# A second level of seven-product multiplication for two of the seven products of the values, in a fused cross-attention, self-attention and expert block

## The chip, the cores and the metric

The kernel runs on one core of a Trainium2 chip, in one launch, with all data in float32. The metric is the device time of one execution in microseconds (us); the number to compare is the median of three runs. The engines are PE (TensorE, with its weight loads as PEld), DVE (VectorE), ACT (ScalarE), POOL (GpSimd) and the DMA queues that SP feeds.

## What is computed

The reference is a block of three layers on 128 latent tokens of width 512, with a context of 12544 tokens of width 512. Cut to what matters here:

```python
# layer 1: quantised self-attention of the latents and cross-attention over the context
kvx = einsum('bsi,oi->bso', cond, w_kv_x)        # cond: 12544 x 512, w_kv_x: 2048 x 512
kx, vx = split(kvx, 2, axis=-1)                  # 8 groups of 128 each
kx = layernorm(kx.reshape(b, sc, 8, 128))
xout = gqa(qx, kx, vx)                           # 16 heads of 128, softmax over 12544 tokens
x = x + proj(concat(core, xout))
# layer 2: causal self-attention of the latents, 16 heads of 32
x1n = ln(ln(x)); x = x + softmax(mask(q k^T)) v Wo
# layer 3: 32 experts, the best 8 of each token, weighted
y = x + moe(ln(x))
```

Nearly all the work is keys and values of the context (`kvx`) and the attention over them.

## The kernel before, in words

**Chunks.** The context is taken in 25 chunks (`chunks`, `NCH`): 24 of 512 tokens and one of 256, which is number 12. For each chunk the kernel makes keys `KT` (8 groups of 128 rows by 512 tokens) and values `V` (4 tiles of 128 tokens by 1024 columns), then scores, an online softmax and outputs. The loop at L856 runs over the chunks. In the scores stage it goes through the eight groups: `scores` (L698: four matmuls per group, 128 x 256 each, copied from PSUM by ACT with the keys' norm as a factor, then a maximum by DVE), and with each group one step of the values of the same chunk. In the keys stage (`keys`, L425) it goes through eight steps of the keys of the next chunk, and after each the outputs of one group (`outputs`, L800).

**Seven products.** Keys and values are made by a multiplication of 2 x 2 blocks in seven products in place of eight. Tokens of a chunk are halved in number and in width (b11, b12, b21, b22), the weights likewise. `mix_tokens` (L284) makes the sums and differences of token blocks on POOL, four operations of 128 x 512 a chunk, one chunk ahead; `mix_weights` makes those of the weights once. Products are numbered by their place in `mixed_w` and `mixed[c]`. `unit` (L319) makes a quarter of the rows: bank `a` takes product 0, then 5, then 6, then 3 on top of each other, `b` takes 1, `c` takes 4 and then 2. ACT copies the sums out of `a` between (`held`: p1, u2, u3), DVE adds. Its four steps are

```python
mm(a, 0, True); p1 = held("p1"); mm(b, 1, True)      # d11 = b + p1
mm(a, 5, False); u2 = held("u2"); mm(c, 4, True)
mm(a, 6, False); u3 = held("u3")                     # d22 = c + u3
mm(a, 3, False); mm(c, 2, False)                     # d21 = a, d12 = c + u2
```

A unit of the values (`v_unit`, L371, matmuls at L378) has two matmuls of 128 x 128 by 512 columns per product; a chunk has two such units, so eight steps, one with each group of scores. A unit of the keys (`k_unit`, L351, matmuls at L359) has four matmuls of 256 columns per product, and there are two a chunk. The banks a, b, c come from `ps_kv`, three PSUM banks in a ring; scores and outputs share three banks of another pool.

**The norm of the keys.** After each unit of keys `k_sums` (L386) squares the unit's rows on ACT, two groups of heads at a time (128 x 1024), into one buffer `sq`, and DVE reduces each half (L395). `k_rstd` then makes the factors for the score copies (a matmul L407, DVE L412, a power on POOL L414).

**The softmax.** `maxima` (L849) runs after each step: at steps 4 and 8 `max_rows` makes the running maxima for four groups on DVE, and at 5, 6, 9 and 10 `spread` (L771) takes two groups: DVE spreads shift and rescale over the rows (L766), subtracts (L783), ACT takes Exp in place (L787), and POOL multiplies the running output `ol` by the rescale (L789) and adds the weights up (L797).

**Order.** Instructions are written in the order of the loops; the framework's planner reorders them within each engine's queue by its own estimate of when they can start. `tc.issue_after(x)` holds an instruction behind another. Each queue runs in order, and each instruction waits there for what it needs. Pools of tiles set which buffers are reused, and so which waits arise.

**The tail.** After the last chunk the outputs are normalised and projected (`proj`), then the self-attention follows (from about L1010): norm (`norm_rows`, L200), four transposes into one PSUM bank (`transposed`, L248), projections for q, v and k in this order, score products L1065 onto a mask already in PSUM, then for four blocks a maximum and a subtraction on DVE, Exp on ACT, transposes, a copy and the value products. `spin` (L931) issues small matmuls of 240 columns whose results nobody reads; the tail has some of these between steps. The router and the experts come last.

Of the kernel before, what the change touches and what calls it, by code (L numbers as in the profile page):

```python
# [17 lines left out]
P = 128  # L18
H = 512
# [26 lines left out]
def block_kernel(  # L46
# [153 lines left out]
    def norm_rows(dst, src, twice=False):  # L200

        st = small.tile([P, 6], F32, tag="st1", name="st1")
        mv = small.tile([P, 2], F32, tag="mv1", name="mv1")
        nc.vector.bn_stats(st, src)
        nc.vector.bn_aggr(mv, st)


        v = small.tile([P, 1], F32, tag="ve1", name="ve1")
        if twice:
            nc.vector.tensor_scalar(v, mv[:, 1:2], 1.0 + EPS, EPS * EPS, ALU.mult, ALU.add)  # L210
        else:
            nc.gpsimd.tensor_scalar(v, mv[:, 1:2], EPS, None, ALU.add)
        rs = small.tile([P, 1], F32, tag="rs1", name="rs1")
        powered[0] = nc.gpsimd.tensor_tensor(rs, v, mhalf[:, :1], ALU.pow).ins
        end = nc.vector.tensor_scalar(dst, src, mv[:, 0:1], rs, ALU.subtract, ALU.mult)
        return end.ins
# [31 lines left out]
    def transposed(pool, src):  # L248

        ps = pool.tile([P, 4, S], F32, tag="ps", name="ps_t")  # L250
        for k in range(4):
            turned[0] = nc.tensor.transpose(ps[:, k, :], src[:, k * P : (k + 1) * P], ident).ins
        return ps

# [48 lines left out]
    mixed, last_mm, added = {}, [None], [None]  # L303
# [15 lines left out]
    def unit(mm, view, d11, d12, d21, d22):  # L319
# [7 lines left out]
        def held(name):  # L327
            t = tmpk.tile([P, CH], F32, tag="u", name=name, bufs=3)
            nc.scalar.copy(view(t), va)  # L329
            return view(t)  # L330
# [54 lines left out]

    def k_sums(c, u):  # L386

        n = chunks[c][1]
        r = tmpk.tile([P, 4, CH // 32], F32, tag="sqr", name="sqr")
        for j in range(2):  # L390
            g = 4 * u + 2 * j
            sq = tmpk.tile([P, 2, CH], F32, tag="sq", name="sq", bufs=1)
            nc.scalar.activation(sq[:, :, :n], KT[:, g : g + 2, :n], AF.Square)  # L393
            for i in range(2):
                nc.vector.tensor_reduce(  # L395
                    r[:, 2 * j + i, : n // 32], sq[:, i, :n].rearrange("p (b i) -> p b i", i=32),
                    AX.X, ALU.add, apply_transpose=True,
                )
        return r
# [284 lines left out]

    olp = late.enter_context(tc.tile_pool(name="olp", bufs=1, side="right", reuse_waits="tile"))
# [10 lines left out]
    prob, mxr, mrun, shifts, lsum, summed = {}, {}, {}, {}, {}, [None]  # L696

    def scores(c, g):  # L698
# [4 lines left out]
        for t0 in range(0, nt, 2):  # L703
            ps = ps_so.tile([P, 2, HS], F32, tag="s", name="s_ps")
            for t in range(t0, t0 + 2):
                end = nc.tensor.matmul(  # L706
                    ps[:, t - t0, :], lhsT=KT[:, g, t * P : (t + 1) * P],
                    rhs=qxT[:, 2 * g : 2 * g + 2, :], start=True, stop=True,
                )
            for t in range(t0, t0 + 2):  # L710
                nc.scalar.activation(  # L711
                    s[:, t, :], ps[:, t - t0, :], AF.Copy, scale=rs[:, t : t + 1]
                )
# [57 lines left out]
    def spread(c, j):  # L771
# [5 lines left out]
        if c:  # L777
            alb = tmp.tile([P, 2, HS], F32, tag="al", name="al", bufs=3)
            to_all(alb, al)
        for a in range(2):  # L780
            g = 2 * j + a
            s = prob[g]
# [4 lines left out]
            nc.scalar.activation(s[:, :nt, :], s[:, :nt, :], AF.Exp, scale=scale)  # L787
            if c:
                nc.gpsimd.tensor_tensor(  # L789
                    ol[g], ol[g], alb[:, a, None, :].to_broadcast([P, 2, HS]), ALU.mult  # L790
# [58 lines left out]
    def maxima(c, i):  # L849

        if i in (4, 8):
            max_rows(c, i // 2 - 2, 2)
        if i in (5, 6, 9, 10):
            spread(c, i // 4 * 2 - 2 + (i - 1) % 4)

    for c in range(NCH):  # L856
# [3 lines left out]
        todo = parts(v_unit(c, v) for v in range(0 if c else 1, chunks[c][1] // HS))  # L860
        for g in range(G):
# [10 lines left out]
            if g == 2 and c + 1 < NCH:  # L872
                with tc.issue_after(summed[0] if c else made):
                    for step in mix_tokens(c + 1):
                        step()

# [11 lines left out]
    with ExitStack() as rest:  # L888
# [7 lines left out]
        stream += [w.rearrange("(k p) o -> p k o", p=P) for w in (aWq, aWv, aWk, aWo)]  # L896
# [113 lines left out]
        with tc.tile_pool(name="po_s", bufs=1, space=PSUM, reuse_waits="tile") as pss:  # L1010
            sps = pss.tile([S, 4, 4, S], F32, name="sps")
            with tc.issue_after(end):
# [8 lines left out]
            pt = transposed(pps, xnn)  # L1021
            xT = post1.tile([P, NK, S], F32, name="xT1")
            for k in range(NK):
                end = nc.vector.tensor_scalar(
                    xT[:, k, :], pt[:, k, :], col("g", k), col("b", k), ALU.mult, ALU.add
# [5 lines left out]
            def project_T(nm, bias, by):  # L1031
                w = next_w()
                ps = pps.tile([P, NK, S], F32, tag="ps", name="ps_qk")
                for j in range(NK):
                    for k in range(NK):
                        nc.tensor.matmul(
                            ps[:, j, :], lhsT=w[:, k, j * P : (j + 1) * P], rhs=xT[:, k, :],
                            start=k == 0, stop=k == NK - 1,
                        )
# [3 lines left out]
                return t  # L1043

            qa = project_T("bq", lambda j: bqs[:, j : j + 1], 1.0 / math.sqrt(AD))
            w = next_w()
            ps = pps.tile([S, H], F32, tag="ps", name="ps_v")
            for k in range(NK):
                nc.tensor.matmul(ps, lhsT=xT[:, k, :], rhs=w[:, k, :], start=k == 0, stop=k == NK - 1)

            va = post1.tile([S, AH, AD + 1], F32, name="va")
            with tc.issue_after(summed[0]):
                nc.gpsimd.memset(va[:, :, AD:], 1.0)
            nc.vector.tensor_tensor(
                va[:, :, :AD], ps.rearrange("s (h d) -> s h d", d=AD),
                bvo[:, 0, :].rearrange("s (h d) -> s h d", d=AD), ALU.add,
            )
            ka = project_T("bk", lambda j: col("bk", j), 1.0)

            for j in range(4):
                for a in range(4):
                    r = slice(a * AD, (a + 1) * AD)
                    end = nc.tensor.matmul(  # L1065
                        sps[:, a, j, :], lhsT=qa[r, j, :], rhs=ka[r, j, :], start=False, stop=True,
                        skip_group_check=True,
                    ).ins
            n = AH // 2 * (AD + 1)
            rest_ps = pss.tile([S, H], F32, name="ps_av2")  # L1070
# [4 lines left out]
            unread = rest_ps[:, H - 240 :]  # L1075

            end = spin(unread, end, 4)
            for a in range(4):
# [3 lines left out]
                nc.vector.tensor_tensor(  # L1082
                    pe, sps[:, a], mx[:, :, None].to_broadcast([S, 4, S]), ALU.subtract
                )
                nc.scalar.activation(pe, pe, AF.Exp)
                with tc.issue_after(end):
                    pt = transposed(pps, pe.rearrange("p j t -> p (j t)"))
                if a in (0, 3):
                    end = spin(unread, turned[0], 1)
# [10 lines left out]
            for i in range(2):  # L1100
# [5 lines left out]
                )  # L1106
            with tc.issue_after(end):
                pt = transposed(pps, av.rearrange("s h d -> s (h d)"))
            end = spin(unread, turned[0], 1)
            avT = post1.tile([P, 4, S], F32, name="avT")  # L1110
            nc.scalar.copy(avT[:, 0:2, :], pt[:, 0:2, :])
            nc.vector.tensor_copy(avT[:, 2:4, :], pt[:, 2:4, :])
# [13 lines left out]
        with tc.tile_pool(name="mo_t", bufs=2, space=PSUM) as mps, tc.tile_pool(  # L1126
# [3 lines left out]
            norm_rows(xn, x2)  # L1130
            with tc.issue_after(end):
                pt = transposed(mps, xn)
            xT = post1.tile([P, NK, S], F32, name="xT2")
            nc.vector.tensor_copy(xT[:, 0:2, :], pt[:, 0:2, :])
            nc.scalar.copy(xT[:, 2:4, :], pt[:, 2:4, :])
# [118 lines left out]
```

## Time and profile before

| | |
|---|---|
| median of 3 runs | 2180.73 us (2180.57 to 2181.01) |
| the profiled execution | 2182.46 us, its span 2180.7 us |
| mean granted TensorE clock | 0.999 |
| one whole chunk, scores to scores (188.50 to 265.51) | 77.01 us |
| its scores stage (419.55 to 458.06, another chunk) | 38.51 us |
| last chunk's outputs begin | 1964.93 us |
| first matmul behind the last projection, tail | 2002.83 us |
| DMA, mean over the span | 44 GB/s |

A row of the page's groups reads: line, engine, operation, output<-inputs, shape, count, then busy time, the mean of one in ns, and the idle time of the engine ahead of it with the instruction that ended most of it. In a timeline the first number is the start and the second the length of a run of like instructions; one matmul of the code shows as two records. In a windows row the first pair is the stretch, then its length, busy time (and instructions) of PE, PEld, DVE, ACT and POOL, the granted TensorE clock, and DMA. A wait reads: who waited for whom, total us, times, longest.

### The profile page before, as it was taken

The page shows a single profiled execution, that of the slowest core. Times are in us where ns is not written, and L with a number is a line of the kernel's source. Part 1 is how long each engine was busy: PE and PEld are TensorE (multiplying, and loading weights), DVE is VectorE, ACT ScalarE, POOL GpSimd, SP SyncE. Part 2 cuts the span into 40 slices and gives each one's busy share as a digit, 9 for nine tenths or more (in the row PEclk, how much of TensorE's full clock was granted, in tenths as well). Part 3 has the DMA queues.
Part 4 walks back from the last instruction along what each step waited for, and adds up shares of the span by engine and source line. Part 5 has one row for each costly group of instructions (what it writes and reads, how often), then busy time and mean ns, then how long its engine had stood idle before and what let it go on. Part 6 is the DMA issues. An engine that isn't in the chain of part 4 may idle for free.

```text
span 2180.7 us, 23767 instructions
## 1 busy us (share of the span) xinstructions
PE 2155.4 (99%) x8671; PEld 1526.5 (70%) x8671; DVE 1307.5 (60%) x2336; ACT 896.3 (41%) x1687; POOL 1092.9 (50%) x1172
## 2 busy tenths in 40 slices
PE   8999999999999999999999999999999999999999
PEld 3667766776776677677776776777677677666554
DVE  8775575567457557646676567557556745757311
ACT  3444454344345434444444345444434434441211
POOL 5233664564476457447574475466456446633000
PEclk9999999999999999999999999999999999999999
DMA  9300000000000000000000000000000000008593
GB/s 319 111 20 1 20 20 1 20 20 20 1 20 20 0 20 20 10 1 20 20 20 17 3 20 20 1 20 20 1 20 20 20 1 20 1 1 276 189 283 116
DMA packets 71221, 95.48 MB, mean 44 GB/s; under 512 B 3136, under 2 KB 39488, under 8 KB 71104
## 3 DMA queue, kind: packets, MB, share of 16 engines
q1 hardware_dynamic: 70816, 93.92, 13.0%
q8 instruction: 68, 1.11, 0.2%
q14 instruction: 49, 0.40, 0.1%
q10 hardware_dynamic: 288, 0.04, 0.0%
HBM read 93.69 MB, written 0.26 MB: 43 GB/s over the span
## 4 chain that ended last, share of the span: by engine, by line
PE 93%; DVE 4%; ACT 1%; DMA 1%; issue 1%; POOL 0%; SPq 0%; POOLq 0%; ACTq 0%; DVEq 0%
PE a_ps L359 15%; PE a_ps L378 15%; PE o_ps L805 15%; PE s_ps L706 15%; PE c_ps L359 8%; PE c_ps L378 7%; PE gu_ps L1169 4%; PE b_ps L378 4%; PE b_ps L359 4%; PE moe_acc L1190 2%; PE ps_p L508 1%; DVE s L783 1%; DVE mxr L717 1%; PE ps_core L668 1%; PE ps_proj L915 1%; DVE m_new L744 1%
## 5 line engine op out<-in xcount | busy, mean ns | idle before, releaser
L797 POOL TENSOR_TENSOR ol<-ol,s 128x256 f32<-128x256 f32 x764 | 550.9, 729 | 58.0 <-ACT s L787 20.3
L711 ACT ACTIVATE s<-s_ps,krs 128x256 f32<-128x256 f32 x784 | 324.1, 471 | 181.4 <-PE s_ps L706 179.2
L414 POOL TENSOR_TENSOR krs<-kve,mhalf 128x16 f32<-128x16 f32 (+1 forms) x50 | 142.8, 2856 | 498.6 <-DVE kve L412 498.6
L789 POOL TENSOR_TENSOR ol<-ol,al 128x512 f32<-128x512 f32 x192 | 242.4, 1273 | 288.8 <-DVE al L766 288.8
L706 PE MATMUL s_ps<-qxT,KT 128*128 128x256 f32 x1568 | 373.1, 381 | 1.6 <-ACT s L711 1.6
L805 PE MATMUL o_ps<-s,V 128*128 128x256 f32 x1568 | 370.7, 379 | 0.0
L706 PEld LDWEIGHTS s_ps<-qxT,KT 128*128 128x128 f32 x1568 | 295.7, 190 | 103.8 <-issue 68.4
L717 DVE TRANSPOSE_TENSOR_REDUCE mxr<-s 128x32 f32<-128x1024 f32 (+1 forms) x200 | 242.4, 1212 | 187.8 <-ACT s L711 184.9
L805 PEld LDWEIGHTS o_ps<-s,V 128*128 128x128 f32 x1568 | 297.1, 190 | 40.8 <-issue 0.5
L787 ACT ACTIVATE s<-s 128x1024 f32<-128x1024 f32 (+1 forms) x200 | 208.1, 1041 | 156.0 <-DVE s L783 150.2
L783 DVE TENSOR_TENSOR s<-s,b_ps 128x1024 f32<-128x1024 f32 (+1 forms) x200 | 230.3, 1171 | 0.0
L329 ACT COPY u<-a_ps 128x512 f32<-128x512 f32 (+1 forms) x198 | 114.5, 578 | 248.8 <-PE a_ps L359 202.3
L378 PE MATMUL a_ps<-wkv,ctx 128*128 128x512 f32 x392 | 186.2, 597 | 1.7 <-DMA ctx<-in_ctxT 1.7
L359 PE MATMUL a_ps<-ctx,wkv 128*128 128x256 f32 (+1 forms) x800 | 185.7, 375 | 1.2 <-POOL ol L789 1.2
L810 DVE TENSOR_TENSOR ol<-ol,o_ps 128x256 f32<-128x256 f32 x192 | 79.7, 415 | 175.6 <-PE o_ps L805 173.5
L359 PEld LDWEIGHTS a_ps<-ctx,wkv 128*128 128x128 f32 x800 | 150.0, 190 | 30.9 <-issue 12.1
L395 DVE TRANSPOSE_TENSOR_REDUCE sqr<-sq 128x16 f32<-128x512 f32 (+1 forms) x200 | 128.0, 678 | 57.4 <-ACT sq L393 57.3
L393 ACT ACTIVATE sq<-KT 128x1024 f32<-128x1024 f32 (+1 forms) x100 | 104.0, 1040 | 134.4 <-DVE KT L348 91.2
L348 DVE TENSOR_TENSOR KT<-c_ps,u 128x512 f32<-128x512 f32 (+1 forms) x50 | 34.0, 681 | 140.0 <-PE c_ps L359 140.0
L378 PEld LDWEIGHTS a_ps<-wkv,ctx 128*128 128x128 f32 x392 | 74.9, 191 | 54.5 <-issue 47.2
L359 PE MATMUL a_ps<-mix,wkv 128*128 128x256 f32 (+1 forms) x400 | 97.4, 386 | 3.4 <-ACT u L329 3.4
L378 PE MATMUL a_ps<-wkv,mix 128*128 128x512 f32 x196 | 94.6, 605 | 0.0
(227 smaller groups left out, 2775.0 us busy)
## 6 DMA issues: line engine op xcount, KB each, us to landing
ctx<-in_ctxT SPq DMA_DIRECT2D x23, 1024.0 KB, 5.0
gu<-in_w SPq DMA_DIRECT2D x32, 384.0 KB, 4.8
gu<-in_v SPq DMA_DIRECT2D x32, 384.0 KB, 5.5
dn<-in_w SPq DMA_DIRECT2D x16, 768.0 KB, 5.5
w<-in_wprojT SPq DMA_DIRECT2D x8, 1024.0 KB, 5.7
w<-in_wqxT SPq DMA_DIRECT2D x4, 1024.0 KB, 11.2
w<-in_wqT SPq DMA_DIRECT2D x4, 1024.0 KB, 6.0
wkv<-in_wkvT SPq DMA_DIRECT2D x8, 256.0 KB, 8.2
```

The costliest lines, as they stand in the source:

```text
L359: nc.tensor.matmul(ps[:, j * h : (j + 1) * h], lhsT=w[:, k, (2 * u + j) * D : (2 * u + j + 1) * D], rhs=x[:, k, :], start=first and j == k ...
L378: last_mm[0] = nc.tensor.matmul(ps, lhsT=x[:, k, v * P : (v + 1) * P], rhs=w[:, k, H : 2 * H], start=first and k == 0, stop=k == 1, skip_g ...
L395: nc.vector.tensor_reduce(r[:, 2 * j + i, : n // 32], sq[:, i, :n].rearrange("p (b i) -> p b i", i=32), AX.X, ALU.add, apply_transpose=True,)
L414: nc.gpsimd.tensor_tensor(rs[:, :, :nt], ve[:, :, :nt], mhalf.rearrange("p (g t) -> p g t", g=4)[:, :, :nt], ALU.pow,)
L706: end = nc.tensor.matmul(ps[:, t - t0, :], lhsT=KT[:, g, t * P : (t + 1) * P], rhs=qxT[:, 2 * g : 2 * g + 2, :], start=True, stop=True,)
L711: nc.scalar.activation(s[:, t, :], ps[:, t - t0, :], AF.Copy, scale=rs[:, t : t + 1])
L717: nc.vector.tensor_reduce(mxr[g // 4][:, g % 4, :nt, :].rearrange("p t k -> p (t k)"), s[:, :nt, :].rearrange("p t (k i) -> p (t k) i", i=32),
L783: nc.vector.tensor_tensor(s[:, :nt, :], s[:, :nt, :], ps[:, a, None, :].to_broadcast([P, nt, HS]), ALU.subtract,)
L787: nc.scalar.activation(s[:, :nt, :], s[:, :nt, :], AF.Exp, scale=scale)
L789: nc.gpsimd.tensor_tensor(ol[g], ol[g], alb[:, a, None, :].to_broadcast([P, 2, HS]), ALU.mult)
L797: summed[0] = nc.gpsimd.tensor_tensor(ol[g][:, 1, :], first, s[:, t, :], ALU.add).ins
L805: end = nc.tensor.matmul(ps, lhsT=V[:, t, g * D : (g + 1) * D], rhs=s[:, t, :], start=t == 0, stop=t == nt - 1,)
```

## The change

For whole chunks other than the first (23 of the 25), the values are made by `v_chunk` in place of two `v_unit`s. Products 1 and 3 appear in one block of the result each. `v_chunk` makes both, for the chunk's two token tiles at once, by seven products of quarter blocks: per quarter product one matmul of 256 columns for product 1 and one for product 3, side by side in a bank. Their four steps run beside groups 0 to 3, and their results go to `V`. Then each of the two token tiles has the other five products in two steps beside groups 4 to 7, and DVE adds their sums to what stands in `V`. The quarter sums of the weights (`finer`, four POOL operations once) and of the tokens (`fx`, eight POOL operations on 128 x 128 a chunk, one buffer, issued in the code after group 4) are new.

To hold these tiles, `k_sums` squares one group of heads at a time (128 x 512) in a buffer of half the size, and the rescale tiles `al` have two buffers in place of three. `spread` is cut in two: the Exp, the rescale and the sums are now in `weigh`, which in chunks 0, 11 and 12 is held behind the last ACT copy at some places, or put off by one step.

In the tail the order of the projections is q, k, then two of v's four matmuls, the score products, and the other two of v; the bias add of v moves behind the first subtraction; three groups of transposes go to two banks in place of one (`transposed_halves`); six of the spins are dropped; and one step of `norm_rows` moves from POOL to DVE.

```diff
-            nc.gpsimd.tensor_scalar(v, mv[:, 1:2], EPS, None, ALU.add)
+            nc.vector.tensor_scalar(v, mv[:, 1:2], EPS, None, ALU.add)
...
+    def transposed_halves(tiles, src):
+
+        for i, ps in enumerate(tiles):
+            for k in range(2):
+                j = 2 * i + k
+                turned[0] = nc.tensor.transpose(
+                    ps[:, k, :], src[:, j * P : (j + 1) * P], ident
+                ).ins
+        return tiles
...
+    def mix_finer_tokens(c, eng):
+        t = finp.tile([P, 2, 4, P], F32, tag="fx", name=f"finer_{c}")
+        finer_x[c] = []
+        for i, x in enumerate((mixed[c][1], mixed[c][3])):
...
+            eng.tensor_tensor(t1, b12, b11, ALU.subtract)
+            eng.tensor_tensor(t2, b22, t1, ALU.subtract)
+            eng.tensor_tensor(t3, b22, b12, ALU.subtract)
+            eng.tensor_tensor(t4, b21, t2, ALU.subtract)
...
+    def v_chunk(c):
...
+        def fine(ps, n, first):
+            for i in range(2):
+                nc.tensor.matmul(
+                    ps[:, i * H // 2 : (i + 1) * H // 2], lhsT=xs[i][n], rhs=f[n][:, i, :],
+                    start=first and i == 0, stop=True, skip_group_check=True,
+                )
...
+        a, b = bank("fa_ps"), bank("fb_ps")
+        fine(a, 0, True)
+        p1 = held(a, "p1")
+        fine(b, 1, True)
+        nc.vector.tensor_tensor(to(0, 0), both(b), both(p1), ALU.add)
+        yield
+        fine(a, 5, False)
+        u2 = held(a, "u2")
+        d = bank("fc_ps")
+        fine(d, 4, True)
+        yield
+        fine(a, 6, False)
+        u3 = held(a, "u3")
+        nc.vector.tensor_tensor(to(1, 1), both(d), both(u3), ALU.add)
+        yield
+        fine(a, 3, False)
+        nc.scalar.copy(to(1, 0), both(a))
+        fine(d, 2, False)
+        nc.vector.tensor_tensor(to(0, 1), both(d), both(u2), ALU.add)
+        yield
+        for v in range(2):
...
+            t1, t2 = V[:, v, :], V[:, 2 + v, :]
+            a, d = bank("a_ps"), bank("c_ps")
+            mm(a, 0, True)
+            nc.vector.tensor_tensor(t1[:, :H], a, t1[:, :H], ALU.add)
+            mm(d, 4, True)
+            nc.scalar.copy(t2[:, H:], d)
+            yield
+            mm(a, 5, False)
+            u2 = held(a, "u2")
+            mm(d, 2, False)
+            nc.vector.tensor_tensor(t2[:, :H], d, u2, ALU.add)
+            mm(a, 6, False)
+            nc.vector.tensor_tensor(t2[:, H:], a, t2[:, H:], ALU.add)
+            added[0] = nc.vector.tensor_tensor(t1[:, H:], a, t1[:, H:], ALU.add).ins
+            yield
...
-        for j in range(2):
-            g = 4 * u + 2 * j
-            sq = tmpk.tile([P, 2, CH], F32, tag="sq", name="sq", bufs=1)
-            nc.scalar.activation(sq[:, :, :n], KT[:, g : g + 2, :n], AF.Square)
-            for i in range(2):
...
+        for j in range(4):
+            sq = tmpk.tile([P, CH], F32, tag="sq", name="sq", bufs=1)
+            nc.scalar.activation(sq[:, :n], KT[:, 4 * u + j, :n], AF.Square)
+            nc.vector.tensor_reduce(
...
-            alb = tmp.tile([P, 2, HS], F32, tag="al", name="al", bufs=3)
-            to_all(alb, al)
+            rescale[j] = tmp.tile([P, 2, HS], F32, tag="al", name="al")
+            to_all(rescale[j], al)
...
+    def weigh(c, j, after=None):
...
+            with tc.issue_after(after) if after else nullcontext():
+                nc.scalar.activation(s[:, :nt, :], s[:, :nt, :], AF.Exp, scale=scale)
...
+            last = copied[0]
+            if c == 0 and i == 6:
+                weigh(c, 0, last)
+            if c == NCH // 2 and i == 10:
+                weigh(c, 2, last)
+            spread(c, j)
+            if (c, j) in ((0, 0), (NCH // 2, 2)):
+                return
+            weigh(c, j, last if (c, j) in ((0, 3), (NCH // 2 - 1, 2)) else None)
...
+        if whole(c):
+            todo = v_chunk(c)
+        else:
+            todo = parts(v_unit(c, v) for v in range(0 if c else 1, chunks[c][1] // HS))
...
+                    if c == 0:
+                        mix_finer_weights(nc.gpsimd)
+            if g == 4 and c + 1 < NCH and whole(c + 1):
+                mix_finer_tokens(c + 1, nc.gpsimd)
...
-        stream += [w.rearrange("(k p) o -> p k o", p=P) for w in (aWq, aWv, aWk, aWo)]
+        stream += [w.rearrange("(k p) o -> p k o", p=P) for w in (aWq, aWk, aWv, aWo)]
...
+            with tc.issue_after(end):
+                end = v_part(range(2))
+            with tc.issue_after(end):
+                for j in range(4):
+                    for a in range(4):
...
+            with tc.issue_after(end):
+                end = v_part(range(2, NK))
...
-            end = spin(unread, end, 4)
...
+                if a == 0:
+                    with tc.issue_after(sub.ins):
+                        nc.vector.tensor_tensor(
+                            va[:, :, :AD], ps_v.rearrange("s (h d) -> s h d", d=AD),
+                            bvo[:, 0, :].rearrange("s (h d) -> s h d", d=AD), ALU.add,
+                        )
...
-                if a in (0, 3):
-                    end = spin(unread, turned[0], 1)
+                end = spin(unread, turned[0], 1) if a == 0 else turned[0]
...
-            end = spin(unread, turned[0], 1)
```

## The prediction

> **What bounds the kernel now.** I read the page first (busy shares, chain), then the timeline of PE over one whole chunk, then PE's waits, then ACT, DVE and POOL in the same chunk by timeline, groups and windows, and last the tail.
>
> ```profile
> PE 2155.4 (99%) x8671; PEld 1526.5 (70%) x8671; DVE 1307.5 (60%) x2336; ACT 896.3 (41%) x1687; POOL 1092.9 (50%) x1172
> PE 93%; DVE 4%; ACT 1%; DMA 1%; issue 1%; POOL 0%; SPq 0%; POOLq 0%; ACTq 0%; DVEq 0%
> ```
> TensorE is busy for all but 25 us, and 93% of the chain that ends last is PE. Ends of matmuls are modelled, so I take rates from starts:
>
> ```profile
> 419.55 1.89 PE L706 MATMUL s_ps<-qxT,KT 128*128 128x256 f32 x8
> 421.27 1.88 PE L378 MATMUL a_ps<-wkv,ctx 128*128 128x512 f32 x4
> 422.99 1.88 PE L378 MATMUL b_ps<-wkv,ctx 128*128 128x512 f32 x4
> 424.71 1.89 PE L706 MATMUL s_ps<-qxT,KT 128*128 128x256 f32 x8
> ```
> One matmul of the code is two records here. Start to start, four records of 512 columns take 1.72 us and eight of 256 take 1.72 us: 0.43 and 0.215 us a record. Half the columns cost half the time. The groups follow without a gap: PE is the bound, and in a normal chunk (419.55 to 496.57, 77.0 us) nothing else holds it. Only a few waits exist, none in a normal chunk:
>
> ```profile
> PE a_ps L359 <- ACT u L329: 3.4, 2, 2.3
> ...
> PE s_ps L706 <- ACT s L711: 1.6, 2, 1.3
> PE a_ps L359 <- POOL ol L789: 1.2, 1, 1.2
> ```
> By the timeline they lie in chunk 0 (1.26 and 1.13), in the turn from chunk 11 to 12 (1.22) and in chunk 12 (0.38 and 2.25), 6.2 us in all. The one put down to POOL has ACT's copy of u at its end (1005.14 to 1005.49, the product starts at 1005.64), behind an Exp.
>
> **The products.** A whole chunk's values are 2 units of 7 products of 2 matmuls of 512 columns. Products 1 and 3 go: 2 units x 2 products x 2 matmuls = 8 of 512 columns, 16 records x 0.43 = 6.88 us. The seven products of quarters are 7 x 2 matmuls of 256 columns: 28 records x 0.215 = 6.02 us. Saved 0.86, or 0.84 with the 1.715 a product that 445.75 to 449.18 gives for two; 23 chunks are whole and not the first: 19.3 us off the bound. That the small form runs at this rate is the row of the scores: same 128 rows, 256 columns, a new stationary tile for every matmul.
>
> **What feeds and empties them.** PE's two halves of the scores stage change length. Now:
>
> ```profile
> core 0: us, PE busy (x) PEld busy (x) DVE busy (x) ACT busy (x) POOL busy (x), PEclk, DMA share, GB/s
> 419.55:438.86 19.31, 19.31 (x70) 11.47 (x68) 10.33 (x15) 10.20 (x22) 2.90 (x1) 1.00 0.00 0
> 438.86:458.06 19.20, 19.19 (x62) 11.32 (x61) 16.87 (x28) 12.30 (x25) 12.98 (x16) 1.00 0.00 1
> ```
> After: heads 0 to 3 have 4 scores x 1.72 + 6.0 + 0.3 = 13.2 us, heads 4 to 7 have 4 x 1.72 + 10 products x 1.72 = 24.1 us. ACT's copies stay eight a chunk. DVE's adds go from six to eleven:
>
> ```profile
> L343 DVE TENSOR_TENSOR V<-c_ps,u 128x512 f32<-128x512 f32 x49 | 33.0, 673 | 5.8 <-ACT u L329 5.8
> L393 ACT ACTIVATE sq<-KT 128x512 f32<-128x512 f32 x4 | 2.5, 631 | 2.8 <-DVE sqr L395 1.8 <-DVE KT L348 1.0
> L797 POOL TENSOR_TENSOR ol<-ol,s 128x256 f32<-128x256 f32 x764 | 550.9, 729 | 58.0 <-ACT s L787 20.3
> ```
> 5 x 0.68 = 3.4 us of DVE, all in the second half: 16.9 + 3.4 = 20.3 of 24.1 us (84%, now 88%); the first half keeps 10.3 in 13.2 (78%). ACT has about 10.6 of 13.2 in the first half (80%, now 53%). Nobody exceeds PE, so the adds are counted at nothing; the cover is PE's longer second half, and without it they would cost up to 3.4 us a chunk. The tight places, one by one: product 5 waits for the add out of its bank, but product 4 and the next scores (3.44 us) lie between, against 0.68 plus one or two DVE operations of 1.2. Product 6 waits for the copy of u2 with only product 2 (1.72) between, against 0.15 + 0.58, or 1.79 with an Exp (1.06) ahead: 0.1 late at worst. The bank of the first unit's product 6 is next needed by product 4 of the second, 3.44 us on, against two adds of 0.68 and a subtraction of 1.19.
>
> The squares are the most exposed. Now:
>
> ```profile
> 399.36 1.06 ACT L393 ACTIVATE sq<-KT 128x1024 f32<-128x1024 f32 x1 [1.87 <-DVE KT L348]
> 402.16 1.06 ACT L393 ACTIVATE sq<-KT 128x1024 f32<-128x1024 f32 x1 [1.74 <-DVE sqr L395]
> 403.13 0.57 ACT L329 COPY p<-a_ps 128x512 f32<-128x512 f32 x1
> ```
> After, one buffer of half the size makes four squares and four reductions take turns: in chunk 12, where squares have 512 columns, square to reduction is 0.66 and reduction's end to the next square 0.10; with a reduction of 0.69 a turn is 1.45. Three turns and the last square (0.53) start p's copy at 399.36 + 4.88 = 404.24; it ends at 404.82. Product 5 that needs it starts at 405.34. Queued behind the squares on ACT are that copy and, at the chunk's turn, the scores' copies; PE waits for both. There the smaller products need p at about 424.7 against about 424.3. So 0 if the turns go as worked out, and up to 1.2 us a chunk if each waits for one more DVE operation. I take 0.13 us, near the computed slack: 3 us over 23 chunks. A gain is excluded here, since the chain only gets longer.
>
> POOL gets eight operations on 128x128 a chunk; none is in the trace; 729 ns for 256 columns and 1273 for 512 make about 0.46 (0.3 to 0.73), 3.7 us. They need the last small product of the chunk before (one buffer) and are read a chunk later. POOL now idles 10.2 us until 443.66, in front of the first rescale, so they cost nothing; in another place they would move the sums, which have 12.8 and 10.2 us of such idle time a chunk. The four weight sums (128x512, 5.1 us) come once, in a POOL gap of 45 us before 123. The Trainium skill speaks against this (SBUF — State Buffer, "SBUF: two separate sides"): a GpSimd operation and a VectorE operation with two SBUF inputs lock each other out for a whole instruction. The trace shows something like it: L749 on DVE took 0.19 us at 441.60 with POOL idle, and 0.70 at 461.07 beside POOL's sums; the three small ones behind it stayed at 0.19. By the rule four small DVE operations wait 0.46 each, 1.8 us; by the row one does, 0.5. Either delays only the first spread, whose Exps end by 448.5 while the first output reads them at 461.5: nothing on PE. The third al buffer goes: it is reused two spreads later, when POOL's rescale is long past. 0.
>
> **The Exps held back** (chunks 0, 11, 12) put the late copies ahead of them, which is what the five waits lack. Between 0 and -6.2; I take -4, as an Exp put off is late elsewhere.
>
> **The tail.** Now the four V matmuls lie ahead of the second projection, and the score products wait for that projection's copy; after, two V matmuls lie between projection and score products and two behind these:
>
> ```profile
> 2014.76 3.73 PE L1036 MATMUL ps_qk<-xT,w 128*128 128x128 f32 x32
> 2018.95 1.28 PE L1065 MATMUL sps<-T_bk,T_bq 32*128 32x128 f32 x32 [0.46 <-ACT T_bk L1042]
> 2020.16 1.89 PE L935 MATMUL ps_av<-qxT,ident 128*128 128x240 f32 x8
> ```
> V (3.43 us) is now wholly ahead of DVE's first maximum (2020.30); after, 1.72 of it is, and the wait of 0.46 is hidden: -2.2 us. The bias add (0.69) moves into DVE's softmax row: +0.7. Transposes in two banks let copies start earlier, three times about 0.3: -0.9. The variance step on DVE saves POOL's 0.24 and a handover: -0.2. The stream's swapped loads land before use (5.7 us each, issued over 15 us ahead): 0. Sum -2.6. Six spins fall. The skill (TensorE: Matmul & The Clock Gate, "What's actually happening") puts the slow clock after an idle window of about 3.4 us, which the change never leaves: by it the spins' removal is free. But here:
>
> ```profile
> 2040.00:2042.00 2.00, 1.48 (x10) 1.11 (x9) 0.42 (x1) 0.37 (x1) 0.00 (x0) 1.00 0.00 0
> 2042.00:2044.00 2.00, 2.00 (x7) 1.33 (x7) 1.24 (x8) 0.77 (x2) 0.00 (x0) 0.55 0.00 0
> ```
> the clock fell to 0.55 with no PE gap over 0.56 us. Two slices at 0.55 and 0.60 cost 1.7 us. The shorter tail may lose this drop (-1.7) or gain another (+1.7). The row decides: the tail lies between -5 and +1; I take -2.6.
>
> **Sum.** -19.3 + 3.0 - 4.0 - 2.6 = -22.9. The profiled execution took 2182.5 (span 2180.7, 1.8 around it), so it would take 2159.6; the median of the runs is 1.7 lower, 2180.7, and becomes 2157.8.
>
> **Rivals.** (1) The new waits are real: the work on ACT in the first half (80%) and the turns of the squares hold PE for 0.5 us a chunk, 11.5 in place of 3: about 2166, up to 2176 at 0.9. For it: the slack of 0.4 to 0.5; against: every product's cover is over 1.7 us. (2) Only the products count; the held-back Exps and the tail give nothing: 2180.7 - 19.3 + 3 = 2164. (3) Slower: the squares' single buffer. If each of its three turns finds DVE in one more operation (0.42 to 1.25 us), p's copy comes 1.3 to 3.7 us later, less 0.5 slack; two such places a chunk. From 0.66 us a place (46 places, 30.4 us, against the 25.9 of the rest) the kernel is slower by 0.2%; at 0.8 it is +37 - 26 = +11, 2192. Against it: DVE is idle for over 1 us on either side of the reductions at 400 and 478. (4) That small products don't pay, since each matmul has a floor: the scores' row excludes it at 256 columns.
>
> **Chances.** Forecast (waits under 0.3 us a chunk) 60%, 2149 to 2163; rivals 1 and 2 together 25%, 2163 to 2176; no change 5%; rival 3 10%. The range 2149 to 2174 leaves out the slow end of rival 1, no change, rival 3 and a little below. About 0.2% (4.4 us) is what a measurement of this kernel can tell from no change: faster 0.85, same 0.05, slower 0.10.
>
> **What would show it.** Right: a chunk of about 76.2 to 76.4 us from scores to scores; the small products at 0.86 us each for four records; PE without waits on u, p or V; POOL's small operations inside its gap; DVE's maximum in the tail 2 to 3 us nearer to the second projection. Wrong: waits of PE for p or s in each chunk, with squares on ACT just before (rival 3 or 1), or adds to V late behind subtractions.

## The result and the profile after

The kernel after takes 2187.3 us (median of 9 runs, 2183.95 to 2189.23) against 2181.0 (9 runs, 2180.43 to 2183.91) before: ratio 1.0026, 95% interval 1.0018 to 1.0034. It is slower, and the forecast of 2157.8 with its range of 2149 to 2174 misses it by some 30 us. The mean granted clock of single runs lies between 0.996 and 1.0 and the time goes with it (after: 2183.95 at 1.0, 2187.84 to 2189.23 at 0.997), so small differences below are also read between runs at 1.0.

The profiled execution took 2187.3, its span 2185.5. The page's busy shares, and below them each engine's share of the chain that ended last:

```profile
PE 2131.1 (98%) x8935; PEld 1580.4 (72%) x8935; DVE 1366.0 (63%) x2452; ACT 923.4 (42%) x1787; POOL 1174.9 (54%) x1359
PE 79%; DVE 13%; ACT 4%; issue 2%; DMA 1%; POOL 0%; SPq 0%; ACTq 0%; POOLq 0%; DVEq 0%
```
PE is busy for 24 us less than before, as meant, yet only 79% of the chain is PE (93% before). The first line of PE's waits says who has taken its place:

```profile
PE a_ps L484 <- ACT u L444: 29.5, 23, 1.3
```
Its columns are the total, the times and the longest. The wait is new: 23 times, once in each whole chunk, on the copy `u` that ACT makes in `v_chunk`'s `held` (L444). PE's timeline shows where:

```profile
440.75 1.88 PE L484 MATMUL a_ps<-wsum,mix 128*128 128x512 f32 x4
442.47 1.88 PE L484 MATMUL c_ps<-wsum,ctx 128*128 128x512 f32 x4
445.63 1.98 PE L484 MATMUL a_ps<-wkv,ctx 128*128 128x512 f32 x4 [1.28 <-ACT u L444]
447.45 1.89 PE L824 MATMUL s_ps<-qxT,KT 128*128 128x256 f32 x8
```
These are products 5, 2 and 6 of the first token tile. From product 2 to product 6 it takes 3.16 us in place of 1.72, and product 6 itself 1.82 until the next start (its restart, 0.10 more than usual): 1.55 us lost, of which the list of waits shows 1.28, because the ends of matmuls are modelled. ACT's timeline of the same microseconds:

```profile
441.12 1.57 ACT L829 ACTIVATE s<-s_ps,krs 128x256 f32<-128x256 f32 x4
442.92 2.19 ACT L912 ACTIVATE s<-s 128x1024 f32<-128x1024 f32 x2 [0.23 <-DVE s L900]
445.01 0.57 ACT L444 COPY u<-a_ps 128x512 f32<-128x512 f32 x1
```
Product 5 ends at about 442.6 and the four score copies at 442.69; the copy of u2 could have run then. But it stands in ACT's queue behind both Exps of the first pair of groups as well, and the first Exp waits for a subtraction on DVE until 442.92. So the copy starts 2.3 us late. The two halves of the scores stage (columns as in the windows row of before):

```profile
420.53:433.87 13.34, 13.34 (x70) 11.48 (x69) 8.56 (x12) 10.50 (x23) 3.52 (x3) 1.00 0.00 1
433.87:459.49 25.62, 24.34 (x74) 13.59 (x72) 21.98 (x39) 12.71 (x25) 19.15 (x27) 1.00 0.00 1
```
Predicted were 13.2 and 24.1. The first is right to 0.1, the second longer by the 1.55.

| from start to start, us | before | after | difference |
|---|---|---|---|
| a whole chunk | 77.01 | 77.34 | +0.33, in each |
| chunk 11 (67.06) and 12 (53.31) | 120.64 | 120.37 | -0.3 |
| scores of chunk 1 to scores of chunk 24 | 1737.92 | 1744.51 | +6.6 |
| last chunk, scores to outputs | 38.51 | 38.95 | +0.4 |
| last outputs to the first matmul behind the projection | 37.90 | 39.51 | +1.6 |
| from there to the experts' first matmul | 38.26 | 36.63 | -1.6 |
| from there to the end of the span | 139.6 | 137.4 | -2.1 |

The differences from the third row on sum to +4.9; the spans differ by 4.8, the rest is rounding. Three of them have a fall of the clock in them: the +1.6 lies in the changed kernel's profile at 1999.4 to 2003.4, one in the same profile at about 2037 to 2041 is in the -1.6, and the -2.1 is mostly the slices at 0.55 and 0.60 of before. The expectation of `tail` below counts before's stretch to 2042.18 (39.35 us) and so leaves out a first matmul of the experts at 2041.09.

### The profile page after: what moved, and what is told of

Same layout as the page of the kernel before. It is cut to its first block, busy times and chain, and to the rows that moved or that the text cites. A ratio compares the mean times of both kernels' runs of the same rounds, so it can differ in the third digit from the quotient of the medians.

```text
span 2185.5 us, 24702 instructions
## 1 busy us (share of the span) xinstructions
PE 2131.1 (98%) x8935; PEld 1580.4 (72%) x8935; DVE 1366.0 (63%) x2452; ACT 923.4 (42%) x1787; POOL 1174.9 (54%) x1359
## 4 chain that ended last, share of the span: by engine, by line
PE 79%; DVE 13%; ACT 4%; issue 2%; DMA 1%; POOL 0%; SPq 0%; ACTq 0%; POOLq 0%; DVEq 0%
PE a_ps L369 15%; PE o_ps L930 15%; PE s_ps L824 11%; PE c_ps L369 8%; PE a_ps L484 7%; PE gu_ps L1327 4%; PE b_ps L369 4%; PE c_ps L484 4%; DVE mxr L835 3%; PE fa_ps L449 3%; ACT s L912 2%; PE moe_acc L1348 2%; DVE m_new L862 2%; DVE mx L852 2%; DVE s L900 2%
## 5 line engine op out<-in xcount | busy, mean ns | idle before, releaser
L484 PE MATMUL a_ps<-wkv,ctx 128*128 128x512 f32 x368 | 175.3, 599 | 29.5 <-ACT u L444 29.5
L512 DVE TRANSPOSE_TENSOR_REDUCE sqr<-sq 128x16 f32<-128x512 f32 (+1 forms) x200 | 138.9, 694 | 87.5 <-ACT sq L511 87.3
L511 ACT ACTIVATE sq<-KT 128x512 f32<-128x512 f32 (+1 forms) x200 | 124.8, 624 | 158.8 <-DVE KT L358 90.8
L369 PEld LDWEIGHTS a_ps<-ctx,wkv 128*128 128x128 f32 x800 | 150.0, 190 | 29.4 <-issue 10.5
L339 ACT COPY u<-a_ps 128x512 f32<-128x512 f32 (+1 forms) x106 | 60.8, 574 | 202.5 <-PE a_ps L369 197.7
L484 PEld LDWEIGHTS a_ps<-wkv,ctx 128*128 128x128 f32 x368 | 68.0, 190 | 105.9 <-issue 55.0
L876 ACT ACTIVATE als<-als 128x32 f32<-128x32 f32 x48 | 11.0, 229 | 200.5 <-DVE als L875 200.5
```

What stands on the lines that cost most here:

```text
L369: nc.tensor.matmul(ps[:, j * h : (j + 1) * h], lhsT=w[:, k, (2 * u + j) * D : (2 * u + j + 1) * D], rhs=x[:, k, :], start=first and j == k ...
L484: last_mm[0] = nc.tensor.matmul(ps, lhsT=x[:, k, v * P : (v + 1) * P], rhs=w[:, k, H : 2 * H], start=first and k == 0, stop=k == 1, skip_g ...
L512: nc.vector.tensor_reduce(r[:, j, : n // 32], sq[:, :n].rearrange("p (b i) -> p b i", i=32), AX.X, ALU.add, apply_transpose=True,)
```

## The experiments

**Theory A**: the wait on u2, an order of ACT's queue, is the whole loss; without it the products would pay. **Rivals**: DVE's new adds delay the subtractions and with them the Exps; the squares' single buffer costs (the prediction's rival 3); the tail or the held-back Exps cost or give less than thought.

**The Exps behind the copy** (`hold`). The changed kernel, with the Exps of the first pair held behind u2's copy, as chunks 0 and 11 have it for other pairs:

```diff
-            nc.scalar.copy(t, a)
+            copied[0] = nc.scalar.copy(t, a).ins
...
-            weigh(c, j, last if (c, j) in ((0, 3), (NCH // 2 - 1, 2)) else None)
+            held = (c, j) in ((0, 3), (NCH // 2 - 1, 2)) or (whole(c) and j == 0)
+            weigh(c, j, last if held else None)
```


> The changed kernel, with the two Exps of the first pair of groups of a whole chunk held behind ACT's copy of u2; same work, other order on ACT. Theory A (the copy's place in ACT's queue is the whole loss): PE's 23 waits of 1.28 us go, 29.5 us and about 0.1 us of restart each, a chunk takes 76.0 us, the kernel 2155 to 2160. Theory B (VectorE and ScalarE are too full in the second half of the scores stage, the wait only shows there): the time lost moves to other waits of PE for adds, Exps or banks, and less than half comes back, the kernel stays above 2172.

Measured: 2152.47 (4 runs, 2148.24 to 2153.11), before 2181.97, ratio 0.9862 (0.9849 to 0.9876), a little better than the 2155 to 2160 expected. No wait on u is left, and a chunk takes 75.79 us. ACT's timeline of this kernel, in one of its whole chunks:

```profile
438.00 0.59 ACT L444 COPY u<-a_ps 128x512 f32<-128x512 f32 x1
438.48 2.01 ACT L912 ACTIVATE s<-s 128x1024 f32<-128x1024 f32 x2
```
and PE's beside it:

```profile
437.74 1.88 PE L484 MATMUL c_ps<-wsum,ctx 128*128 128x512 f32 x4
439.46 1.88 PE L484 MATMUL a_ps<-wkv,ctx 128*128 128x512 f32 x4
```
The copy runs as soon as product 5 (436.03 to about 437.8) and the score copies (to 437.97) are done, and product 6 follows product 2 in 1.72. The one run of each kernel at clock 1.0 puts them 2183.95 - 2148.24 = 35.7 us apart, which is 23 x 1.55. Nothing else was changed, and all of DVE's new adds are still there, so the order of these three instructions on ACT is the loss.

**One Exp ahead, not two** (`one`). `hold`, but only the second Exp is held:

```diff
-            with tc.issue_after(after) if after else nullcontext():
+            with tc.issue_after(after) if after and (a or not second) else nullcontext():
                 nc.scalar.activation(s[:, :nt, :], s[:, :nt, :], AF.Exp, scale=scale)
```


> The version with the Exps of the first pair held behind the copy u2, but only the second of the two Exps is held; the first (1.06 us) may stand ahead of the copy again. Theory A (the cost of the change is what stands ahead of u2 in ACT's queue, an Exp at a time, together with the subtraction that each Exp waits for): product 6 starts 0.4 to 0.5 us late from start to start, the list of waits shows product 6 on u again in each of 23 whole chunks with 0.2 to 0.4 each, and the time is about 10 us above the held version's 2152.5: 2160 to 2164. The prediction's own number for one Exp (0.1 late, 0.1 x 23 = 2.3 us) would give 2154 to 2155. A rival, that the wait appears only where both Exps stand ahead, gives the held version's time, 2151 to 2153, and no wait on u.

Measured: 2162.14 (4 runs, 2159.25 to 2163.33), ratio 0.9904 (0.989 to 0.9919). A chunk takes 76.21, 0.42 more than with none ahead; 23 x 0.42 = 9.7, and 2162.14 - 2152.47 = 9.7. ACT's timeline of this kernel:

```profile
439.00 1.06 ACT L912 ACTIVATE s<-s 128x1024 f32<-128x1024 f32 x1 [0.23 <-DVE s L900]
439.97 0.57 ACT L444 COPY u<-a_ps 128x512 f32<-128x512 f32 x1
```
PE's of the same stretch, products 2 and 6:

```profile
438.55 1.88 PE L484 MATMUL c_ps<-wsum,ctx 128*128 128x512 f32 x4
440.58 1.98 PE L484 MATMUL a_ps<-wkv,ctx 128*128 128x512 f32 x4 [0.15 <-ACT u L444]
```
And its list of waits:

```profile
PE a_ps L484 <- ACT u L444: 2.4, 15, 0.2
```
Product 6 is 0.31 late and its own restart 0.11: not the 0.1 of the prediction, which had left out the 0.23 for which the Exp waits, and the restart. The list shows a quarter of it, and in 15 chunks only (0.2 to 0.4 in each of 23 were expected there), though by the starts product 6 comes 2.0 us behind product 2 in every one of the 23.

**Without DVE's first add** (`noadd`). The changed kernel, leaving out the add of product 0 in the first token tile (the output lacks that term there):

```diff
             mm(a, 0, True)
-            nc.vector.tensor_tensor(t1[:, :H], a, t1[:, :H], ALU.add)
+            if v:
+                nc.vector.tensor_tensor(t1[:, :H], a, t1[:, :H], ALU.add)
```


> The changed kernel without VectorE's add of product 0 into the values of the first token tile (its half of these values lacks that product). Theory A: the Exps ahead of the copy of u2 wait for VectorE's subtractions, so they and the copy come 0.6 us earlier; PE's wait falls from 1.28 to about 0.65 us, the kernel by 14 us to about 2173. If the wait comes from ScalarE's own load and not from what VectorE has to do first, it stays at 1.28 and the time at 2187.

Measured: 2187.15 (9 runs), ratio 1.0024 (1.0014 to 1.0034); a chunk takes 77.28. The expectation of 2173 missed. The first Exp did come 0.6 us earlier (1.56 us behind product 5's start in place of 2.17), but the planner then put two of the score copies between the two Exps, as ACT's timeline of this kernel shows (the second Exp, 443.65, is left out):

```profile
441.97 1.06 ACT L913 ACTIVATE s<-s 128x1024 f32<-128x1024 f32 x1 [0.96 <-DVE s L901]
442.93 0.82 ACT L830 ACTIVATE s<-s_ps,krs 128x256 f32<-128x256 f32 x2
...
444.59 0.58 ACT L444 COPY u<-a_ps 128x512 f32<-128x512 f32 x1
```
The two score copies took back what the add had cost, and everything that stood ahead of the copy still stands ahead of it. So this run doesn't price the add, and its time of 2187, which the expectation had kept for ScalarE's own load as the cause, doesn't prove that either. The trace of the changed kernel bounds it: the Exps' waits for DVE are the 0.23 shown and some 0.2 before the second (the pair takes 2.19 there, 2.01 in `hold`), 0.4 of the 2.3 us; the rest is the Exps themselves. And in `hold` all adds stand and no wait is left.

**Product 6 later** (`split`). The changed kernel with ACT's order left alone and PE's changed: product 6 of the first tile goes one step on, behind the next group's scores, and the second tile's five products follow in the last steps:

```diff
...
             mm(0, a, 5, False)
             u2 = held(a, "u2")
             mm(0, d, 2, False)
             nc.vector.tensor_tensor(t2[:, :H], d, u2, ALU.add)
+            yield
             mm(0, a, 6, False)
...
```


> The changed kernel with its products in another sequence on PE: product 6 of the first token tile comes one step later, behind the scores of the next group, together with product 0 of the second tile; ACT's order stays, the two Exps are still ahead of the copy of u2. Theory A (what counts is the work PE has between product 5 and product 6 against ACT's queue ahead of u2): the scores' 1.73 us cover the 1.45 us, PE waits for u no more, a chunk takes 75.8 us, 2150 to 2155, like the run with the Exps held. Theory B (holding the Exps helped by spacing the subtractions, additions and Exps that follow, not by the copy alone): the time stays above 2170.

Measured: 2161.75 (4 runs, 2160.43 to 2165.09), ratio 0.991 (0.9894 to 0.9926). Both Exps are still ahead of the copy (Exps at 439.13, copy at 441.23), and nobody waits for u: the scores cover it. That half of the expectation held; the 2150 to 2155 did not. The second tile's adds now end the stage, and PE's next unit of keys needs their bank; from this kernel's list of waits:

```profile
PE b_ps L369 <- DVE V L517: 6.9, 12, 1.3
```
Chunks take 75.87 or about 76.55. The wait on u has become a wait on `V` in 12 of the 23 chunks; the more exact cure is the order on ACT. Which 12 can be read from DVE, where four small operations run ahead of that add. One of them in a chunk without the wait (first line), and two in a chunk where PE waits 0.56:

```profile
453.30 0.60 DVE L889 TENSOR_TENSOR sh<-m_new,qb 128x32 f32<-128x32 f32 x1
528.95 0.76 DVE L887 TENSOR_TENSOR m_new<-m_new 128x32 f32<-128x32 f32 x1
529.75 0.77 DVE L889 TENSOR_TENSOR sh<-m_new,qb 128x32 f32<-128x32 f32 x1
```
Where POOL is idle, each takes up to 0.19. Here they run beside POOL's sums, and the two long ones last as long as the sum of that time (528.94 to 529.66, 529.74 to 530.47). In exactly the 12 chunks that wait two of the four take over 0.7; in the 11 others only one is long, at 0.6.

**The new products alone** (`prod`). The kernel before with `v_chunk`, the finer sums, the small squares and two `al` buffers, the Exps of the first pair held behind u2, and no other edit:

```diff
...
+            last = copied[0]
+            spread(c, j)
+            weigh(c, j, last if whole(c) and j == 0 else None)
```


> The kernel before with nothing but the new products of the values in whole chunks (with the finer sums, the small squares and the second buffer that they need), the two Exps of the first pair held behind u2; no edit of the tail, no held-back Exps in chunks 0, 11 and 12. Theory A (the products save 1.2 us a chunk when u2 is in time, and the other edits give next to nothing on the median): 23 x 1.2 = 28 us faster than before, 2153 to 2156, ratio about 0.987 to 0.989, a chunk of 75.8 us against 77.0. Rival: the held version's gain came in good part from the tail and the special chunks; then above 2160.

Measured: 2154.26 (4 runs, 2152.56 to 2155.92), before 2182.62, ratio 0.987 (0.9854 to 0.9887); a chunk takes 75.79. At clock 1.0 it is 2180.8 - 2152.6 = 28.2 us, and 23 x (77.01 - 75.79) = 28.1. The gain of `hold` is in the products.

**The small squares alone** (`ksums`). The kernel before with the squares by one group of heads and a buffer of half the size:

```diff
-            sq = tmpk.tile([P, 2, CH], F32, tag="sq", name="sq", bufs=1)
-            nc.scalar.activation(sq[:, :, :n], KT[:, g : g + 2, :n], AF.Square)
+            sq = tmpk.tile([P, CH], F32, tag="sq", name="sq", bufs=1)
+            nc.scalar.activation(sq[:, :n], KT[:, 4 * u + j, :n], AF.Square)
```


> The kernel before, with only the squares of the change: four squares of 128x512 and four reductions taking turns on one buffer, in place of two and two. Theory A: no cost, the copy of p behind them still ends before PE needs it, 2181 +- 2. The rival named in the prediction (the squares' turns hold PE): at 0.66 us a place 2211, and PE waits for p or s in every chunk.

Measured: 2181.51 (12 runs, 2180.01 to 2184.32), ratio 0.9999 (0.9991 to 1.0008). Rival 3 falls, and the 3.0 us taken for the squares were 0; `hold` and `prod`, which have them beside the new products, show no wait for them in a whole chunk either.

**The held-back Exps alone** (`exps`). The kernel before with `weigh`, its rules for chunks 0, 11 and 12 and two `al` buffers, and nothing else.

```diff
-            nc.scalar.activation(s[:, :nt, :], s[:, :nt, :], AF.Exp, scale=scale)
...
+            with tc.issue_after(after) if after else nullcontext():
+                nc.scalar.activation(s[:, :nt, :], s[:, :nt, :], AF.Exp, scale=scale)
```

> The kernel before, with only the Exps held back in chunks 0, 11 and 12 (and the third buffer of the rescale gone). From the waits seen in the changed kernel: five waits of PE of together 5.4 us in place of five of 6.2 us, so 0.8 us faster, 2181 +- 1; by the prediction 4 us faster, 2178.

Measured: 2180.62 (12 runs, 2178.8 to 2180.89), before 2181.91, ratio 0.9992 (0.9983 to 1.0): some 1.3 us, at the edge of what can be told. Its list of waits has lost those for u and the longer one for s, and has waits for `KT` (1.5 us in two) and for p (1.3) in their place; the one put down to POOL's `ol` is 1.4 (1.2 before).

**The tail alone** (`tail`): the kernel before with the order of q, k and v, the late bias add, the transposes in two banks, the norm's step on DVE and the six spins gone. From its edits:

```diff
-            qa = project_T("bq", lambda j: bqs[:, j : j + 1], 1.0 / math.sqrt(AD))
+            qa, end = project_T("bq", lambda j: bqs[:, j : j + 1], 1.0 / math.sqrt(AD))
+            ka, end = project_T("bk", lambda j: col("bk", j), 1.0, end)
...
-            end = spin(unread, turned[0], 1)
+            end = turned[0]
```
**The tail with spins put back** (`spins`): `tail` with spins again behind the transposes of two blocks and of the result.

```diff
-                end = spin(unread, turned[0], 1) if a == 0 else turned[0]
+                end = spin(unread, turned[0], 1) if a in (0, 1, 3) else turned[0]
...
-            end = turned[0]
+            end = spin(unread, turned[0], 1)
```


> The kernel before, with only the edits of the tail: the order of the projections, the transposes in two banks, six spins fewer, the norm's step on VectorE. Theory A: 2 to 4 us faster, 2177 to 2179, from the first mask matmul to the first expert 36.6 us in place of 39.35. Rival: fewer spins let the TensorE clock fall once more in the tail, which costs 1.7 us a time; then 0 to 1 us faster or a little slower, and more spread between runs.

> The kernel before, with the edits of the tail and the same three spins put back. Theory A: the gain of the new order in the tail shows, median 2176 to 2179, clock 0.999 or more in most executions. If the clock falls as in the run with the tail's edits alone, 2181 to 2183.

Measured: `tail` 2182.39 (13 runs, 2176.51 to 2182.68), ratio 0.9998 (0.9989 to 1.0006); `spins` 2179.14 (21 runs, 2177.3 to 2183.59), ratio 0.9989 (0.9982 to 0.9995). The only run of `tail` at clock 1.0 took 2176.51, about 4 us under the runs of before at that clock (2180.0 to 2180.65); but 12 of its 13 runs were below 1.0, 11 of them at 0.998 or less. Two windows of `tail`'s profiled run, whose third number from the end is the clock:

```profile
2028.00:2032.00 4.00, 4.00 (x18) 3.59 (x17) 0.79 (x3) 0.07 (x1) 0.00 (x0) 0.50 0.06 22
2032.00:2036.00 4.00, 3.58 (x8) 1.75 (x7) 0.90 (x3) 0.37 (x1) 0.00 (x0) 0.52 0.01 4
```
With the three spins back, on the same chip, 18 of 21 runs are at 0.999 or 1.0, and those at 1.0 take 2177.3 to 2177.8; the kernel before stood at 0.999 or 1.0 in 26 of 30 runs beside `tail` and in 31 of 32 beside `spins`. So the tail's reordering is worth about 4 us by that one run, the clock takes it back in the runs without the spins, and three spins cost about 1 us of it. That the spins hold the clock up is what these counts speak for; how they would do it, no run shows.

**A version that beats both** (`best`): `hold` with the three spins.

> The run with the Exps held, with spins put back into the tail: one each behind the transposes of blocks 1 and 3 and one behind the transposes of the attention's result. Theory A (fewer spins let the TensorE clock fall in the tail): mean clock 0.999 or 1.000 in most executions, median 2148 to 2150. If the clock falls anyway, 2151 to 2153 as before.

Measured: 2151.88 (4 runs, 2150.87 to 2153.0), ratio 0.9864 (0.985 to 0.9878), 1.4% faster than before; not to be told from `hold` on four runs each. The expected 2148 to 2150 missed: two runs are at 0.999 and two at 0.998. In its profiled run the clock fell in the stretch where `tail`'s did, with all three spins in place and no listed gap of PE over 0.3 us in the 5 us ahead of it:

```profile
1996.00:2000.00 4.00, 4.00 (x18) 3.65 (x18) 0.00 (x0) 1.17 (x2) 0.00 (x0) 0.50 0.47 166
```
So the three spins make this fall rarer at most; they do not exclude it.

## Why the prediction was wrong

- **Products** (-19.3): right, and more. A quarter product is 0.86 us for four records, as the scores' row said. Without the wait a chunk is 1.22 us shorter, of which the products are 0.82 by start to start. The rest was not seen: in each whole chunk of before, product 3 of the second token tile started 1.90 us after the scores ahead of it in place of 1.72, and the next one 1.82 later. From PE's timeline of before:

```profile
452.62 1.89 PE L706 MATMUL s_ps<-qxT,KT 128*128 128x256 f32 x8
454.52 1.98 PE L378 MATMUL a_ps<-wkv,mix 128*128 128x512 f32 x4
```
And from ACT's:

```profile
452.21 1.06 ACT L787 ACTIVATE s<-s 128x1024 f32<-128x1024 f32 x1 [0.53 <-DVE s L783]
453.17 0.82 ACT L711 ACTIVATE s<-s_ps,krs 128x256 f32<-128x256 f32 x2
453.88 0.58 ACT L329 COPY u<-a_ps 128x512 f32<-128x512 f32 x1
```
That is 0.18 + 0.10 = 0.28 us a chunk. By the times it hangs on a copy of u3 that stands behind an Exp and score copies and ends at 454.46 (no run moved this copy alone). The prediction said that nothing but PE's work holds PE in a normal chunk; no list shows this wait, since the modelled end (1.89) covers it. The sign was there: a copy covered by one group of scores already came late behind an Exp. The keys stage gave 0.13 more (38.51 to 38.38): there too, starts of before at 463.24 and 471.95 come just behind copies that end at 463.07 and 471.81, the second behind two Exps.
- **Waits** (+3.0): wrong, 35.7. The step that failed is "Product 6 waits for the copy of u2 with only product 2 (1.72) between, against 0.15 + 0.58, or 1.79 with an Exp (1.06) ahead: 0.1 late at worst." The place was right, the bound was not: the Exps come in pairs, 2 x 1.06, and each waits for DVE besides. One Exp costs 9.7 us in all, two cost 35.7: the cover is used up by the first, and what follows counts in full. By the prediction's own numbers the second Exp makes 1.79 into 2.85, 1.1 over the cover of 1.72; it was never put into the sum. The 3 us taken for waits were put on the squares, which cost 0. Rival 1 had the kind of the loss and the wrong place and size; no rival had 1.5 us a chunk at u2.
- **Adds** (0): right for `hold`, where all eleven stand and no matmul waits. In the changed kernel they lie in the way of the subtractions, at most 0.4 us of the copy's 2.3, which the prediction didn't follow. DVE has 30.5 us in the two halves, as predicted (30.6), but 21.98 of it in the second (20.3 predicted).
- **POOL** (0): right. The eight operations on 128 x 128 took 0.45 each, at 433.25 to 436.6, with POOL idle again until 441.8. DVE's four small operations stayed at 0.17 to 0.19, but at 439.76 and 460.51, when POOL was idle, so the delay weighed in the prediction was not met here. `split` met it: one or two of the four lasted as long as a sum of POOL (0.73), between the one and the four that were weighed, and there it reached PE.
- **Held-back Exps** (-4): about -1. The waits moved from u and s to p and `KT` and became little shorter: in those chunks 4.6 us are listed in `exps` and 5.4 in the changed kernel, against 6.2 before.
- **Tail** (-2.6): about -4 without the clock, 0 with it. From the projection to the end of the span `hold`, with the clock at 1.0, takes 172.6 us and the profile of before 177.9, of which its two slow slices are 1.7; that leaves 3.6, and `tail`'s one run at 1.0 shows 3.8. The rule of the Trainium skill weighed in the prediction (TensorE: Matmul & The Clock Gate, "What's actually happening") would have made the removed spins free; the row of before's clock at 0.55 spoke against it, and the runs are with the row: 11 of 13 of `tail` at 0.998 or less, 3 of 21 of `spins`, and `best` with the clock at 0.50 behind gaps of no more than 0.3 us. In the profile of after the clock fell twice, between 1999.4 and 2003.4 in the projection, where 24 records took 12.2 us in place of 10.5, and from about 2037 to 2041, with this window in it:

```profile
2038.00:2040.00 2.00, 2.00 (x5) 0.97 (x4) 0.42 (x1) 0.00 (x0) 0.00 (x0) 0.50 0.00 0
```
The clock stands at 0.50 there with PE busy throughout.

The sum by what was measured, at clock 1.0: products and what went with them -28.1, u2 +35.7, tail about -4, Exps about -1: +2.6, where the runs have 2183.95 - 2180.4 = +3.6. The other 2 to 3 us between the medians go with the clock. What makes it fall in one run and not in another stays open; so does the 1 us left in this sum.

## What to carry to other kernels

A short copy that stands between two matmuls of one bank is priced by all that the planner may put ahead of it on its engine, and by what those instructions wait for, not by one of them; if a product is to follow early, hold the long work behind the copy by hand. Look for such places by the distance from start to start of equal matmuls: a distance of 1.90 in place of 1.72 can be a wait that no list names. Look then at what ended just ahead of the late start: a group of scores behind the small matmuls of L407 takes 1.83 too, with no wait listed. An edit that saves 0.8 us in each of 23 chunks is worth its order on every queue that it touches, since one misplaced pair cost nearly twice what it saved.

## What the runs showed of the hardware

- A listed wait is not its price: 1.28 listed was 1.55 (the changed kernel), 0.15 listed was 0.42 (`one`), and 0.28 was not listed at all (before). After each such wait the next four records of 512 columns took 1.82 in place of 1.72 us.
- A small DVE operation of 0.19 us took up to 0.77 beside POOL's sums of 0.73, and ended with one of them (`split`, L887 and L889; before, L749 with 0.70).
- The granted clock fell to 0.50 with no listed gap of PE over 0.7 us in the 10 us ahead (the changed kernel at 1999.4 and 2037, `tail` at 2025, `best` at 1995), each time with matmuls of 1 or of 33 columns ahead of it; behind the fall at 2037 eight records of 512 columns took 4.9 us in place of 3.7. In the profile of `hold`, with the clock at 1.0, the same matmuls ran without a fall, so this says where it fell and gives no rule for when.
